# Edge groups visited in twos, windows stored as 24 rows, and the last chunk's node sums formed on chip, in a graph layer on one core

## The chip, the cores and the metric

The kernel runs on one core of one Trainium2 chip. The core has a matrix engine (TensorE, PE in the profile; its weight loads are PEld), a vector engine (VectorE, DVE), an activation engine (ScalarE, ACT), a general engine (GpSimd, POOL), a queue engine (SyncE, SP) and 16 DMA engines that all queues share. Each engine carries out its own instructions in the order in which they stand; between engines there are semaphores. DMAs are issued on the queues of SP, ACT and POOL. The metric is the device time of one execution in microseconds.

## The reference, cut to what matters

```python
xn = layernorm(x)                                   # 10000 nodes x 512, fp32
# graph part: 160000 edges, sorted by dst
h = xn @ W
agg = segment_sum(h[src] * edge_weight[:, None], dst, num_segments=10000)
gnn = relu(agg + bias)
# mixing part: linear attention, 8 heads of 64
q, k, v = split(xn @ w_qkv.T)
q = softmax(q over the head's 64) * 64 ** -0.5      # k: softmax over the nodes
mix = layernorm((q @ (k.T @ v) per head) @ w_out.T) * gamma
x1 = x + gnn + mix
# feed-forward: 6 experts, one set of expert weights for the whole graph
r = router(mean over nodes of layernorm(x1))        # top 2 of 11 partitions
out = x1 + sum_e r[e] * (gelu(layernorm(x1) @ W1[e] + b1[e]) @ W2[e] + b2[e])
```

`dst` is 10000 u^2 for uniform u, so low node numbers have many edges and high ones few. The sum over edges is formed before the product with W, on rows of xn: segment_sum(w * xn[src]) @ W.

## The kernel before

**Chunks.** The nodes are held in NCH = 20 chunks: 19 of 512 rows (128 partitions x SUB = 4 rows) and a last one of 272 (68 partitions x 4). KB = 4 blocks of 128 columns make up the 512.

**Start (0 to about 160 us).** SP loads the chunks of x (`normal_rows`, L416). DVE makes their statistics (L166, L167), POOL and ACT finish and apply them (L422), and ACT stores the rows to `xn_d` in DRAM (L424). After LISTS = 10 chunks the edge lists are loaded, and `place_edges` (a generator of DVE steps) works out which window and row every edge belongs to; two of its steps are taken after each further chunk. Meanwhile PE forms keys and queries of chunks 0 and 1 (L209), DVE their softmax (L192 to L194) and the sums G = xn.T ek (L912, L919). Rows of chunks from 2 on are reloaded from `xn_d` (`rows_of`, L835).

**Edges.** The 160000 edges are NET = 1250 tiles of 128. A window of up to 32 rows (WIN) takes the sums of one tile (of two for the first PAIRED = 384 windows), since tiles of edges sorted by dst touch few nodes. GROUP = 4 windows share one PSUM bank: a group's matmuls (L602) have 32 columns of weights each, side by side, and give `pm` of 128 rows. `edges_in` issues a group's gathers on POOL (L584, 128 rows of xn_d each) and makes its selection matrices on DVE (L590, L592). `edges_summed` does the matmuls, the copy out of PSUM on ACT (L605) and one store of 256 KB to `part_d` on ACT's queue (L606). There are 217 groups (NQ) and buffers for 24 tiles. Two windows that share nodes are joined by `carry` (L674, a DMA that adds in DRAM), chained over stretches whose ends are CARRIES.

**Order of the work.** The order on PE is written out by hand. Between blocks of other matmuls `work(us)` is told how long the block takes, and calls `edges_to` with the number of groups that a fixed rate (PACE, then ROW_PACE) allows by then. `edges_to` first issues gathers ahead (AHEAD, then LATE tiles) and then does the visits. The order on the other engines comes from a scheduler, with ties where the code says `behind(a, b)`.

**Stage 1 (to about 1092 us)** makes keys, queries and G for chunks 2 to 19, with seven products in place of eight (L243), edge groups between. A branch for unusual edge lists follows (`general_path`, not taken here), and the small product that mixes heads.

**Stage 2 (about 1115 to 1906 us).** For every chunk: `attention` (po = q times G, L209, kept as `ot`), then `gathered(c)`, which fetches the chunk's summed rows from part_d by the list `row_of` (L1018 on POOL; a node without edges takes a row of zeros), their transposes (L201, aT), and pg = aT times W (L209). DVE adds the bias, applies relu, adds to `ot` (L1090, L1091) and makes statistics for the feed-forward part; `ot` is stored to x1_d. Attention runs MIXED = 3 chunks ahead. `far_enough` has AT_HAND, which says how many windows must be done and carried before a chunk's rows may be fetched; the last two chunks wait for all edges. At chunk 17 `all_edges_in` does the rest of the edges and the last carry, and loads the experts' weights; DVE then forms w_sum (L226 to L229). After chunk 18 the first rows of the feed-forward part are loaded, normalised (L351 on ACT), transposed (L367 on DVE) and summed to xs (L233 to L236).

**Feed-forward (about 1906 us to the end)** is a long run of L243 products, with sums on DVE and gelu on ACT (L1277, L1290 to L1297).

Of the kernel before, what the change touches and what calls it, by code (L numbers as in the profile page):

```python
# [17 lines left out]
P = 128  # L18
SQ = 32
# [7 lines left out]
WIN = P // GROUP  # L27
FAR = 1.0e5
EARLY = 2
ROWS_IN = 1.6  # L30
LISTS = 10
# [5 lines left out]
LATE = 4  # L37
MIXED = 3

AT_HAND = [(5, 320), (7, 384), (8, 424), (9, 472), (10, 520), (11, 560), (12, 604), (13, 640), (14, 680), (15, 716), (16, 752),  # L40
           (17, 788), (18, 820)]
# [11 lines left out]
]  # L53


@with_exitstack
def gps_layer_kernel(
# [91 lines left out]
    ZERO_ROW = NQ * P  # L149
# [38 lines left out]
    def softmax_rows(q, r, s):  # L188
# [5 lines left out]
        nc.vector.tensor_tensor(q3, q3, qs[:r, :, None].to_broadcast([r, D // HEAD, HEAD]), ALU.mult)  # L194
# [29 lines left out]
    def sums_of(o, a11, a12, a21, a22):  # L224
# [4 lines left out]
        nc.vector.tensor_tensor(o[3], a12, o[1], ALU.subtract)  # L229
# [149 lines left out]
    def sums_of_weights():  # L379
        w1_sb, w1_sum = held_w["w1"], held_w["w1_sum"]  # L380
        p_half, q_half = slice(0, PAIRS * P), slice(PAIRS * P, 2 * PAIRS * P)
        sums_of([w1_sum[:, i] for i in range(4)], w1_sb[:, :KH, p_half], w1_sb[:, KH:, p_half],
# [5 lines left out]
    with ExitStack() as ph:  # L388
# [18 lines left out]
        normal = []  # L407
        placing = []
        last_stats = [None]

        def normal_rows(n):

            for c in range(len(normal), min(len(normal) + n, NCH)):
                r = chunks[c][1]
                xt = (xp if c < KEPT else a_io).tile([P, SUB, D], F32, name="xn")
                nc.sync.dma_start(xt[:r], tokens(x, c))  # L416
# [11 lines left out]
                for _ in range(2 if placing else 0):  # L428
                    next(placing[0], None)
# [10 lines left out]
        count = ep.tile([P, 3 + len(AT_HAND) + 2 * NCH], F32, name="count")  # L440
        small_norms = ep.tile([P, 2, KB], F32, name="small_norms")
        usable = ep.tile([P, 1], F32, name="usable")
        n_odd = ep.tile([1, 1], I32, name="n_odd")

# [9 lines left out]
        def place_edges(dst_sb, row_sb):  # L454


            nc.vector.tensor_scalar(row_sb, row_sb, 2, None, op0=ALU.arith_shift_right)
            yield
# [12 lines left out]
            def by_window_of(t, per_window, o, op):  # L471
# [27 lines left out]
            nc.vector.scalar_tensor_tensor(place, place, float(SUB), good, op0=ALU.add, op1=ALU.subtract)  # L499
            yield  # L500
            nc.vector.scalar_tensor_tensor(good, place, float(SUB), beyond, op0=ALU.is_lt, op1=ALU.is_equal)
            yield
            nc.vector.scalar_tensor_tensor(good, place, float(WIN), good, op0=ALU.is_lt, op1=ALU.mult,
                                           accum_out=count[:, 0:1])
# [3 lines left out]
            nc.vector.scalar_tensor_tensor(good[:, : NW - 1], gap[:, : NW - 1], float(WIN // SUB), good[:, : NW - 1],  # L508
                                           op0=ALU.is_lt, op1=ALU.mult, accum_out=count[:, 1:2])
# [14 lines left out]
        def window_at(node, more):  # L524
            tile_no = NET * (node / N) ** 0.5 + more
            return min(max(int(tile_no / 2 if tile_no < 2 * PAIRED else tile_no - PAIRED), 0), NW)

        def span(c):
            return window_at(chunks[c][0], -SPARE), window_at(chunks[c][0] + SUB * chunks[c][1], SPARE)
# [153 lines left out]

        done = [0, 0.0]
        pace = [PACE]
        ahead = [AHEAD]
        EARLY_TOTAL = PRODUCT * KB * ROWS_IN * 3 * KB

        def edges_to(stop):
# [784 lines left out]
```

## Time and profile before

| what | us |
|---|---|
| median of 3 runs | 3501.84 (3490.08 to 3503.91) |
| the profiled execution | 3295.9, of it the span 3294.2 |
| PE busy | 3187.5 (97%) |
| DVE busy | 1772.1 (54%) |
| POOL busy | 1317.8 (40%) |
| ACT busy | 834.1 (25%) |
| mean granted PE clock | 0.985 of full |

The span is from the first to the last instruction of the profiled execution. The profiled execution took 206 us less than the median of the runs. A busy PE counts from start to modelled end of its records, so 97% says that it rarely stood still, not that it did as much as it could. A record is one pass; a matmul in fp32 leaves two. In a list of waits, the idle time of an engine is put down to the instruction whose semaphore came last. A DMA-issuing line on POOL or ACT shows the time of issue, not that of the transfer.

### The profile page before, as it was taken

Reading aid. Unit: us, or ns where it says so; the run is one execution under the profiler, and the core shown is the slowest. Engines: PE = TensorE matmul, PEld = TensorE weight load, DVE = VectorE, ACT = ScalarE, POOL = GpSimd, SP = SyncE. Lnnn points to the kernel's source line nnn. Section 1 sums busy time; section 2 is a strip of 40 time slices with the busy share of each in tenths; the row PEclk is TensorE's granted clock in tenths of the full one; section 3 lists DMA queues with packets and bytes.
Section 4 is the critical chain, followed back from the end, with each engine's and each line's share of the span. In section 5 each row is a group of like instructions: output and inputs, shape, how many; then the busy total and the mean of one; then the engine's idle time right before and its main releaser. Section 6 shows DMA issues by size and latency. Waiting matters only on the chain. (4 is left out here: it accounts for less than half of the span.)

```text
span 3294.2 us, 35223 instructions
## 1 busy us (share of the span) xinstructions
PE 3187.5 (97%) x12819; PEld 1898.0 (58%) x12819; DVE 1772.1 (54%) x3902; ACT 834.1 (25%) x1674; POOL 1317.8 (40%) x1421
## 2 busy tenths in 40 slices
PE   5899999999999999999999979999999999999998
PEld 3344444444443333333333358888888888888886
DVE  6655555555555366666665665455544554445532
ACT  5422222222222122222222132222222222222211
POOL 3377777777776777777777200000000000000000
PEclk8899999999999999999999989999999999999999
DMA  9678889888888999999999822121212212121111
GB/s 391 245 238 282 265 274 311 265 281 255 283 267 240 344 353 355 337 350 351 354 338 313 230 67 62 52 90 52 64 52 76 66 52 64 52 90 51 54 38 41
DMA packets 216728, 654.33 MB, mean 199 GB/s; under 512 B 34425, under 2 KB 74361, under 8 KB 188831
## 3 DMA queue, kind: packets, MB, share of 16 engines
q0 software_dynamic: 104096, 354.29, 32.9%
q1 hardware_dynamic: 69992, 175.33, 16.2%
q10 hardware_dynamic: 42452, 122.31, 9.6%
q8 instruction: 105, 1.72, 0.2%
q14 instruction: 83, 0.68, 0.1%
HBM read 491.21 MB, written 166.63 MB: 200 GB/s over the span
## 5 line engine op out<-in xcount | busy, mean ns | idle before, releaser
L584 POOL DMA_INDIRECT msg<-xn_d,src_sb x1250 | 1237.6, 990 | 422.9 <-issue 318.4
L602 PE MATMUL pm<-msg,sel 128*32 128x512 f32 x2504 | 357.7, 604 | 15.4 <-DMA msg<-xn_d,src_sb 14.4
L209 PE MATMUL pg<-wq,aT 128*128 128x512 f32 (+1 forms) x640 | 292.2, 604 | 0.0
L209 PE MATMUL po<-G,qT 128*128 128x512 f32 (+1 forms) x640 | 290.3, 600 | 1.4 <-DMA qT<-qT_d 1.4
L912 PE MATMUL pc<-xn,ek 128*128 128x512 f32 (+1 forms) x640 | 285.5, 596 | 0.0
L605 ACT COPY part<-pm 128x512 f32<-128x512 f32 x217 | 127.0, 585 | 618.3 <-PE pm L602 577.4
L602 PEld LDWEIGHTS pm<-msg,sel 128*32 128x32 f32 x2504 | 67.0, 109 | 273.0 <-issue 190.5
L209 PEld LDWEIGHTS pg<-wq,aT 128*128 128x128 f32 (+1 forms) x640 | 115.5, 188 | 176.1 <-issue 161.2
L243 PE MATMUL px<-xnT,w_sb 128*128 128x256 f32 (+1 forms) x800 | 204.9, 379 | 7.0 <-DVE u L1291 6.6
L209 PEld LDWEIGHTS po<-G,qT 128*128 128x128 f32 (+1 forms) x640 | 114.8, 187 | 164.7 <-issue 157.8
L166 DVE BATCH_NORM_STATS2 st<-ot 128x6 f32<-128x512 f32 (+1 forms) x160 | 110.4, 690 | 180.1 <-ACT ot L1053 179.3
L243 PE MATMUL p<-kq_sum,xs_b 128*128 128x512 f32 (+1 forms) x432 | 200.7, 600 | 0.0
L912 PEld LDWEIGHTS pc<-xn,ek 128*128 128x128 f32 (+1 forms) x640 | 118.0, 191 | 139.3 <-issue 131.4
L243 PE MATMUL px<-w_sb,hh 128*128 128x256 f32 (+1 forms) x800 | 185.8, 379 | 0.0
L243 PE MATMUL py<-xs,w_sum 128*128 128x256 f32 (+1 forms) x800 | 185.7, 375 | 0.0
L243 PE MATMUL py<-w_sum,hh 128*128 128x256 f32 (+1 forms) x800 | 179.2, 379 | 0.0
L243 PEld LDWEIGHTS px<-xnT,w_sb 128*128 128x128 f32 x800 | 150.8, 192 | 30.1 <-DVE u L1291 10.2
L243 PEld LDWEIGHTS px<-w_sb,hh 128*128 128x128 f32 (+1 forms) x800 | 150.2, 188 | 22.8
L243 PEld LDWEIGHTS py<-w_sum,hh 128*128 128x128 f32 (+1 forms) x800 | 150.0, 188 | 22.7
L243 PEld LDWEIGHTS py<-xs,w_sum 128*128 128x128 f32 x800 | 150.2, 191 | 20.1
L243 PEld LDWEIGHTS p<-kq_sum,xs_b 128*128 128x128 f32 (+1 forms) x432 | 78.0, 187 | 116.1 <-issue 89.6
L351 ACT ACTIVATE xn<-xn,st_all 128x128 f32<-128x128 f32 x288 | 114.8, 481 | 97.3 <-DMA xn<-x_d 97.3
(298 smaller groups left out, 4566.8 us busy)
## 6 DMA issues: line engine op xcount, KB each, us to landing
part_d<-part ACTq DMA_DIRECT2D x217, 256.0 KB
msg<-xn_d,src_sb POOLq DMA_INDIRECT x1250
xn<-in_x SPq DMA_DIRECT2D x19, 1024.0 KB
xn_d<-xn ACTq DMA_DIRECT2D x19, 1024.0 KB
qT_d<-qT ACTq DMA_DIRECT2D x19, 1024.0 KB
qT<-qT_d SPq DMA_DIRECT2D x19, 1024.0 KB
xt<-in_x SPq DMA_DIRECT2D x19, 1024.0 KB
x_d<-ot SPq DMA_DIRECT2D x19, 1024.0 KB
```

The source lines that it names most:

```text
L166: nc.vector.bn_stats(st[:r, s, :], t[:r, s, :])
L209: nc.tensor.matmul(po[:r, :], t[:, kb, s * r : (s + 1) * r], w[:, kb, :], start=kb == 0, stop=kb == KB - 1)
L243: nc.tensor.matmul(o, lhs[j], rhs[j], start=start and j == 0, stop=stop and j == n - 1, skip_group_check=True)
L351: nc.scalar.activation(xn[:, s, b * P : (b + 1) * P], xn[:, s, b * P : (b + 1) * P], AF.Identity, bias=st[:, b, s, 0:1], scale=st[:, b, s, ...
L584: nc.gpsimd.indirect_dma_start(out=m[k], out_offset=None, in_=xn_d, in_offset=bass.IndirectOffsetOnAxis(ap=src_sb[:, t0 + k : t0 + k + 1], ...
L602: nc.tensor.matmul(pm[h * WIN : (h + 1) * WIN, :], sel[:, k, :], m[k] if k < len(m) else m[0], start=j == 0, stop=j == batch - 1, skip_gro ...
L605: nc.scalar.copy(part, pm)
L912: nc.tensor.matmul(pc, ek[:r, s, cb * P : (cb + 1) * P], xn[:r, s, :], start=s == 0, stop=s == SUB - 1)
```

## The change

Three constants change the edges' rhythm, and two others their limits.

- **Visits in twos.** In stage 2 `edges_to` is called for a multiple of VISIT = 2 groups, and gathers are issued LATE = 8 tiles ahead instead of 4. `limit` holds back the last groups until their place at chunk 17.
- **24 rows stored.** In stage 2 each window's first USED = 24 rows are stored, by four DMAs a group in place of one. `rest_cleared` fills rows 24 to 31 of those windows with zeros once, by 16 stores on ACT's queue early in stage 1. The check of the lists (`place_edges`) now asks for 24 rows in these windows.
- **The last chunk's sums on chip.** Groups from ON_CHIP = 211 on keep their sums in SBUF (`parts`). `last_sums` adds them up for the last chunk, already transposed: a matmul of the parts with 0/1 matrices `mine`, which say which of the last 272 nodes each row belongs to (`numbered`, from an iota on POOL and DVE comparisons with `node_of`, which `nodes_on_chip` makes). What windows before 211 x 4 hold of those nodes is fetched from part_d as before and added in by small matmuls. Only groups up to STORED = 214 are still stored. The last carry (to the last window) goes, and a carry at window 853 is added to AT_HAND for chunk 18.
- **Order at the end of stage 2.** The last chunk's attention comes in its turn. Chunk 17's pg, two visits, the first 16 of the matmuls of `last_sums`, and the last visit follow each other; the gathers of chunks 18 and 19 are tied behind the last gather of edges. Loads of the first feed-forward rows and of the experts' weights move to the end of chunk 17; `sums_of_weights` moves to the end of chunk 18, and the last chunk's additions are tied behind it.
- **Order at the start.** The edge lists are loaded after LISTS = 18 chunks asked for. The first step of `place_edges` is tied behind the last statistics, and the step that ends the places is tied behind the last softmax of chunk 1; the steps are no longer dealt out between chunks. The reload of chunk 2 is tied behind the last load of x.

In the built order, stage 2 has 63 visits (60 of 8 tiles, 2 of 16, 1 of 12) in place of 118 (111 of 4, 5 of 8, one of 16, one of 24). Stage 1's visits and the feed-forward products are the same.

```diff
+USED = 24
-LISTS = 10
+LISTS = 18
-LATE = 4
+LATE = 8
+VISIT = 2
+FIRST_SUMS = 4
-           (17, 788), (18, 820)]
+           (17, 788), (18, 820), (19, 853)]
...
+    ON_CHIP = window_at(N, NET, chunks[-1][0], -3) // GROUP
+    STORED = -(-CARRIES[-1] // GROUP)
...
-                for _ in range(2 if placing else 0):
-                    next(placing[0], None)
...
-            part = pools["w"].tile([P, D], F32, name="part")
+            if i < ON_CHIP:
+                part = pools["w"].tile([P, D], F32, name="part")
+            else:
+                if (i - ON_CHIP) % 3 == 0:
+                    parts.append(io.tile([P, 3, D], F32, name="parts", tag="qT"))
+                part = parts[-1][:, (i - ON_CHIP) % 3, :]
             nc.scalar.copy(part, pm)
-            nc.scalar.dma_start(part_d[i * P : (i + 1) * P, :], part)
+            if batch > 1:
+                nc.scalar.dma_start(part_d[i * P : (i + 1) * P, :], part)
+            elif i < STORED:
+                for h in range(GROUP):
+                    nc.scalar.dma_start(by_window[i * GROUP + h, :USED, :], part[h * WIN : h * WIN + USED, :])
...
+        def rest_cleared():
+            zero = pools["w"].tile([P, PER, D], F32, name="none", tag="on", bufs=1)
+            nc.gpsimd.memset(zero, 0.0)
+            for w in range(PAIRED, STORED * GROUP, P):
+                end = min(w + P, STORED * GROUP)
+                for q in range(USED, WIN, PER):
+                    nc.scalar.dma_start(by_window[w:end, q : q + PER, :], zero[: end - w])
...
-            edges_to(groups_of(int(done[1] / pace[0])))
+            stop = min(groups_of(int(done[1] / pace[0])), limit[0])
+            edges_to(done[0] + (stop - done[0]) // visit[0] * visit[0])
...
+            if c == KEPT:
+                behind(load, last_load[0])
...
-                for _ in placing[0]:
-                    pass
+                for step in placing[0]:
+                    if step:
+                        behind(step, last_softmax[0])
...
+                behind(next(placing[0]), last_stats[0])
...
         def all_edges_in():
             edges_to(NQ)
-            carry(CARRIES[-1], NW - 1)
+            ats.append(gathered(NCH - 2))
+            ats.append(gathered(NCH - 1))
...
+            rows_first = rows_in(0)
             experts_weights()
...
+        def numbered():
+            b, r = chunks[-1]
+            mine = io.tile([P, NQ - ON_CHIP + 1, SUB, r], F32, name="mine", tag="xt", bufs=1)
+            number = mine[:, NQ - ON_CHIP]
+            nc.gpsimd.iota(number, pattern=[[1, SUB], [SUB, r]], base=b, channel_multiplier=0,
+                           allow_small_or_imprecise_dtypes=True)
+            for g in range(NQ - ON_CHIP):
+                nc.vector.tensor_scalar(mine[:, g], number, node_of[:, g : g + 1], None, op0=ALU.is_equal)
+            return mine
+
+        def last_sums(o, mine, groups, at):
+            n = SUB * chunks[-1][1]
+            for kb in range(KB):
+                kbs = slice(kb * P, (kb + 1) * P)
+                pt = psum.tile([P, SUB * P], F32, name="pt", tag="ps")[:, :n]
+                for g in groups:
+                    nc.tensor.matmul(pt, parts[g // 3][:, g % 3, kbs], mine[:, g].rearrange("p s n -> p (s n)"),
+                                     start=g == groups[0], stop=at is None and g == groups[-1], skip_group_check=True)
+                if at is None:
+                    nc.scalar.copy(o[:, kb, :n], pt)
+                    continue
+                r = chunks[-1][1]
+                for s in range(SUB):
+                    nc.tensor.matmul(pt[:, s * r : (s + 1) * r], at[:r, s, kbs], ident[:r, :r],
+                                     start=False, stop=s == SUB - 1, skip_group_check=True)
+                nc.vector.tensor_tensor(o[:, kb, :n], o[:, kb, :n], pt, ALU.add)
...
+            behind(sums, held["asked"])
...
-            if c + MIXED < NCH - 1:
+            if c + MIXED < NCH:
                 mixed.append(attention(c + MIXED, nodes_rows))
-            elif c == NCH - 3:
-                mixed.append(attention(NCH - 1, nodes_rows))
+            elif c < NCH - 1:
+                nodes_rows()
             else:
-                nodes_rows()
+                last_sums(aT, mine, range(FIRST_SUMS, NQ - ON_CHIP), at)
...
+            if c == NCH - 3:
+                limit[0] = ON_CHIP + FIRST_SUMS
...
+                if c == NCH - 1:
+                    behind(added, weights_summed)
...
             if c == NCH - 3:
-                sums_of_weights()
+                mine = numbered()
+                aT_last = io.tile([P, KB, SUB * P], F32, name="aT_last", tag="ot", bufs=MIXED + 2)
+                edges_to(limit[0])
+                last_sums(aT_last, mine, range(FIRST_SUMS), None)
+                rows_first = all_edges_in()
             if c == NCH - 2:
...
-                turn = turned_in(0, rows_turned(0, xn))
+                turn = turned_in(0, rows_turned(0, rows_first))
+                weights_summed = sums_of_weights()
```

## The prediction

> **What bounds the kernel now.** I read the page's totals first, then the table of stretches, the groups, the timelines of PE and POOL where they stop, and the chain of waits.
>
> ```profile
> PE 3187.5 (97%) x12819; PEld 1898.0 (58%) x12819; DVE 1772.1 (54%) x3902; ACT 834.1 (25%) x1674; POOL 1317.8 (40%) x1421
> L584 POOL DMA_INDIRECT msg<-xn_d,src_sb x1250 | 1237.6, 990 | 422.9 <-issue 318.4
> L602 PE MATMUL pm<-msg,sel 128*32 128x512 f32 x2504 | 357.7, 604 | 15.4 <-DMA msg<-xn_d,src_sb 14.4
> ```
>
> Over the whole span PE is the bound. But 1250 gathers of 0.95 us, with 0.30 us of issue between, are 1563 us in one queue: from the first at 149.5 to the last at 1837.8 POOL does hardly anything else. In that stretch two resources are nearly balanced, and the stretches show where the second one wins (columns: us; busy time of PE, PEld, DVE, ACT, POOL; PE clock; DMA share; GB/s):
>
> ```profile
> 1115.00:1785.00 670.00, 666.69 (x2324) 252.16 (x2324) 411.63 (x1057) 151.68 (x289) 504.62 (x506) 1.00 0.96 347
> 1785.00:1846.00 61.00, 49.18 (x153) 14.66 (x152) 23.57 (x64) 9.39 (x18) 38.43 (x40) 0.89 0.87 286
> 1846.00:1906.00 60.00, 59.50 (x183) 25.97 (x181) 46.12 (x94) 8.38 (x20) 6.30 (x45) 1.00 0.71 183
> 1906.00:1927.00 21.00, 7.98 (x28) 6.75 (x29) 11.62 (x23) 8.57 (x20) 0.00 (x0) 0.67 0.71 175
> ```
>
> From 1785 PE runs dry; the last gather sets the end of stage 2. The timelines (start, length) show that end on POOL and PE:
>
> ```profile
> 1837.81 0.95 POOL L584 DMA_INDIRECT msg<-xn_d,src_sb  x1 [0.30 <-issue]
> 1852.12 0.96 POOL L674 DMA_DIRECT2D part_d<-part_d  x1 [13.36 <-DMA b_sb<-in_b_b]
> 1857.22 1.04 POOL L1018 DMA_INDIRECT at<-part_d,row_of  x1 [4.14 <-DMA part_d<-part_d]
> 1919.02 2.05 PE L243 MATMUL px<-xs,w_sum 128*128 128x256 f32 x4 [13.52 <-DVE xs L235]
> ```
>
> With P the end of the last gather (1838.8), stage 2 ended at 1905.5 = P + 66.7, all PE work, and then came a hole of 13.5 us. The waits of PE name the holes that the change touches:
>
> ```profile
> PE pm L602 <- DMA msg<-xn_d,src_sb: 14.4, 14, 2.6
> PE pt L201 <- DVE G L919: 13.6, 2, 13.2
> PE px L243 <- DVE xs L235: 13.5, 1, 13.5
> ```
>
> **What the Trainium skill says.** "TensorE: Matmul & The Clock Gate", section "Part 1: The HAM clock gate": after an idle window of about 3.4 us the PE clock halves until it has been busy again. The trace agrees: four px records took 2.05 us after the 13.5 us hole, 1.03 later. So a long stall costs about 2 us more. The same page, section "Architectural detail", calls the queues of ACT and DVE strict first in, first out; the trace agrees (L351 stood behind root L174 of the last chunk until 1908.3). "DMA: Bandwidth & Descriptors", section "Why a DMA increments its semaphore by 16 and not by 1", says that a DMA is spread over the largest number up to 16 that divides its slowest dimension: 68 rows use 4 engines. The trace agrees: loading the 68-partition chunk ran alone at 106 GB/s with 0.22 of the engines busy. So a 24-row store would use 12 engines, and four of them put 8 rows on each, as one 128-row store puts on sixteen. Those twelve are not relieved; no run here shows it.
>
> **The change, part by part.** Record times are from PE's timeline, start to start: a 512-column record 0.43 us (two per matmul, so 0.86), a transpose 0.11; a 272-column record by ratio 0.23. The order on each engine is that of the changed program as built.
>
> *Start.* In before, DVE's small place_edges operations stand among statistics, and G L919 came late: the 13.2 us hole at 87. Moved behind the last statistics, they let the softmax and G follow statistics of chunks 16 and 17, whose loads landed at 91 and 94. I get chunk 0 done 7.5 us earlier (4 to 11). The second half, about 7.5 us of DVE (1.44+1.46+1.5+0.6+1+0.5+0.9), now stands ahead of xs_b, which the first L243 needs: at 157.0 in before, needed at 159.6, so it is late by 3.5 to 5. Net -3.5 us (-8 to +3). The reload's tie costs nothing: it is ready 30 us before its transposes. Sixteen clearing stores (7.7 MB, at 370 GB/s 21 us of DMA, 16 issues of 0.33 to 0.5 us on ACT) fall into 131 to 165, where DMA is mostly idle; without that cover they would hold qT copies and PE by up to 6 us.
>
> *POOL.* It gains a memset and four early gathers, but the fifth waits for place_edges' last sums, about 156 to 159, beside 155.9 before. Before, it then filled its 24 buffers and waited 6.2 us for PE's first visits (185 to 220), which now come 3.5 us earlier. So P' = P - 3 (-8 to +6).
>
> *Pairs.* A visit of four tiles costs 1.19 us, one of eight 2.10, so each pair saves 0.29. Stage 2 goes from 118 visits to 63: -15.7 us of PE. *Last sums.* 24 matmuls x 0.456 + 16 x 0.224 - 16 small transposes = +13.4 us. Net -2.3 us of PE, and only where PE is the bound.
>
> *Stores.* 118 groups x 3 more ACT issues x 0.33 to 0.5 us is 117 to 177 us of ACT in 790; it was 23% busy there (151.7 of 670). Hidden by ACT's idle time, if the stores land soon enough (second rival).
>
> *End of stage 2.* `mine` begins with an iota on POOL, placed behind the last gather. DVE's first is_equal waits for it, and behind that on DVE stand the additions and ot of chunk 16's second and third quarters, whose PSUM buffers chunk 17's transposes and pg need. PE gets there after the visit of groups 211 and 212, while 14 gathers (14 x 1.255 = 17.6 us) still have to be issued: it arrives about 8 to 11 us too early. Call the iota's end I; the trace has none of this size, the nearest POOL work is 0.3 to 1.06 us, so I = P' + 1.2 (0.5 to 3). Then: DVE catches up 3.4; pg 6.9; visit 2.1; pg 6.9; 16 La1096 7.3; last visit 2.1: I + 28.7. Chunk 18's sums come last: their last needed store leaves at I + 12.7, lands 5.8 later (as before's last, 1846.3 to 1852.1), then carry 5.1, gather 1 + 4 to 8: I + 28.6 to 32.6, a wait of 0 to 4, I take 1.5. Then transposes 1.75, pg 13.7, pst 0.9, sums 7.2, pg 13.7 = 37.3. One slow-clock stretch adds 2. End = P' + 1.2 + 28.7 + 1.5 + 37.3 + 2 = P' + 70.7, against P + 66.7: +4 (-2 to +12). The work now after the last visit is 30 us shorter; the stall takes that.
>
> *FFN start.* From T, the end of chunk 18's pg: normalising on ACT ends T+7.7, DVE's transposes T+11.6, xs T+14.8, three of four w_sum (1.48 each) T+19.2. PE works until T+22.6, so the 13.5 us hole closes. But the last chunk's additions stand behind w_sum: 8 x 0.64, statistics 3 + 1.4, gate rows 1.9 after T+20.7 or PE's last pg; u is done at T+32.8, and px's third product needs it. So that product starts 10.2 us after the last pg, in before 20.8 (1905.5 to 1926.3), a slow clock and its growth included: -9.7 after 0.9 for the clock (-13 to -3).
>
> Sum: -3 + 4 - 9.7 = -8.7 on 3295.9 us (span 3294.2): 3287. The runs have a median of 3501.84, 206 us above the profiled execution. If that is fixed, the same -8.7 gives 3493. If it is a slower PE, POOL's stalls shrink, and -3.5 - 2.3 - 9.7 gives 3486. I take 3493.
>
> **Rivals.** *Faster: PE, not POOL, sets stage 2.* If gathers run 20 us earlier, the iota is early and pairs pay: before's 1115.2 to 1905.5 less 51.5 us that its visits took beyond 1.19 and 2.10 is 738.8 of PE work; 736.5 from 1111.7, with the 27 us of such waits that came before 1750 and 1.5 for the last sums, ends at 1876.7. With the FFN start that is -38: 3464. For it: in 1100 to 1840 POOL waited 19.6 us (43 times) for earlier gathers, at 0.96 DMA share, and stored bytes fall by a quarter. Against it: the 12 engines, and POOL's rate of 39 to 40 gathers in 50 us was the same at 0.83.
>
> *Slower: stores hold ACT.* Each store waits for the one eight before it, the same store of the previous pair, about 10.5 us back. Copies of pm, aT and po stand behind it on ACT; pm has two buffers. The decisive point is a landing beyond 10.5 us: alone it was 5.8, carries under load took 7 to 11. An excess of 0.8 us in 60 visits is 48, less about 17 of slack that PE has against POOL: +31 - 8.7, so 3524. For it: DMA's 0.96 and 12-engine stores; against: ACT's idle 77%.
>
> *No effect at all of the FFN part* (weights landing late, w1 being loaded behind the last visit): -8.7 + 9.7 gives 3503; it lies inside my range.
>
> **How the numbers follow.** No change can be told from one within about 0.5%, 17.5 us. Likeliest case 0.42 (with its late-weights form), own range 3481 to 3507: 0.05 of it faster. Faster rival 0.38, 3450 to 3484, of it 0.03 same. Slower rival 0.20, 3505 to 3545, of it 0.02 same. Faster 0.05 + 0.35 = 0.40; same 0.37 + 0.03 + 0.02 = 0.42; slower 0.18. The range, 3458 to 3522, leaves out a tenth of each end.
>
> **What would show it.** Right: PE idle 8 to 11 us on DVE ot before chunk 17's pg; the last gather near 1836; stage 2's end about 71 us after it; no hole ahead of the first px, one of about 5 us ahead of its third product; the hole at 87 near 6, and one of 4 at the first L243. Wrong: is_equal finding its iota done; the last gather before 1820 or after 1850; msg waits spread through stage 2; ACT's DMA issues waiting ahead of copies.

## The result, and the profile after

The changed kernel took 3526.2 us (median of 22 runs, 3493.1 to 3547.7); the kernel before, run beside it, 3489.9 (22 runs, 3457.2 to 3508.1). The ratio is 1.0084, 95% interval 1.0063 to 1.0105: slower by about 29 us. (The ratio is formed from fast runs alone, without the two longest executions of the changed kernel; the medians of all runs lie 36 us apart.) The forecast was 3493, range 3458 to 3522.

One thing must be known to read any number below: chips came in two kinds. In the later comparisons the kernel before took 3492 to 3495 us on three chips and 3298 on two, every one of its 20 to 59 runs on a chip within 1% of that chip's median. The profile that the prediction was read from (3295.9) looks like the quick kind, the timed runs beside it (3490 to 3504) like the slow kind. The comparison above is of the slow kind. Each of the five chips was measured at one time only, so the kind may also be a state in which the chip was then.

From the page of the changed kernel: engine totals, and two groups.

```profile
PE 3274.2 (93%) x12883; PEld 1942.7 (55%) x12883; DVE 1773.1 (50%) x3930; ACT 826.3 (23%) x1674; POOL 1314.0 (37%) x1423
...
L594 POOL DMA_INDIRECT msg<-xn_d,src_sb x1250 | 1236.1, 989 | 654.8 <-issue 333.4
L612 PE MATMUL pm<-msg,sel 128*32 128x512 f32 x2504 | 355.3, 612 | 39.4 <-issue 29.1
```

The span is 3527.1 us. The gathers take what they took before (0.99 us each). POOL was idle ahead of them for 655 us, where the profile behind the prediction has 423. But most of that comes with the kind of chip and not with the change, as the page of the kernel before on a chip of the slow kind shows (b_again, below):

```profile
L584 POOL DMA_INDIRECT msg<-xn_d,src_sb x1250 | 1232.4, 986 | 625.3 <-issue 339.6
```

On the slow kind POOL does not set the pace, with or without the change. The list of waits of the changed kernel says for whom it waited, and how PE stood still (total, times, longest):

```profile
PE pt L211 <- issue: 32.4, 36, 3.8
PE pm L612 <- issue: 29.1, 35, 1.5
PE po L219 <- issue: 20.5, 19, 5.4
PE pg L219 <- issue: 20.3, 12, 6.0
...
PE pt L211 <- DVE G L973: 8.6, 1, 8.6
...
POOL msg L594 <- PE pm L612: 145.0, 51, 12.0
```

POOL waited 145 us for PE to give buffers back (110 in b_again). In the trace that the prediction used, PE's waits in stage 2 were for gathers (14.4 us); here they are many waits with no releaser shown ("issue"), spread over transposes, visits and products. The four groups listed come to 102 us; the same four come to 67 in b_again. The hole for G has shrunk from 13.2 to 8.6, as the start of the change meant.

The end of stage 2, from the timelines of POOL and PE (start, length):

```profile
2071.49 0.95 POOL L594 DMA_INDIRECT msg<-xn_d,src_sb  x1 [0.30 <-issue]
2072.45 0.39 POOL L1084 IOTA mine<- 128x272 f32 x1
...
2073.89 0.81 PE L211 MATMUL pt<-ident,at 128*128 128x128 f32 x4 [3.17 <-issue]
2080.95 8.88 PE L219 MATMUL pg<-wq,aT 128*128 128x512 f32 x16 [6.25 <-ACT aT L213]
...
2156.98 2.07 PE L253 MATMUL px<-xnT,w_sb 128*128 128x256 f32 x4 [4.88 <-DVE u L1380]
```

The iota stands behind the last gather, and PE is held for 3.2 and 6.3 us ahead of chunk 17's pg. The last pg ended at 2146.9, and the third px product began 10.1 us later.

Against an execution of the kernel before on a chip of the same kind (span 3492.4), stage by stage from the PE timelines:

| stretch | before | after | difference |
|---|---|---|---|
| first L243 (L253 after) product starts at | 159.4 | 157.1 | -2.3 |
| stage 1, to the first po | 1116.4 | 1118.0 | +1.6 |
| stage 2, first po to the last pg's end | 829.5 | 871.8 | +42.3 |
| last pg to the third px product | 21.6 | 10.1 | -11.5 |
| from there to PE's end | 1354.1 | 1359.1 | +5.0 |

The start and the beginning of the feed-forward part moved about as forecast. The loss is in stage 2.

### The profile page after: what moved, and what is told of

Read it like the earlier page. It is cut to its first block, busy times and chain, and to the rows that moved or that the text cites. A ratio compares the mean times of both kernels' runs of the same rounds, so it can differ in the third digit from the quotient of the medians.

```text
span 3527.1 us, 35757 instructions
## 1 busy us (share of the span) xinstructions
PE 3274.2 (93%) x12883; PEld 1942.7 (55%) x12883; DVE 1773.1 (50%) x3930; ACT 826.3 (23%) x1674; POOL 1314.0 (37%) x1423
## 3 DMA queue, kind: packets, MB, share of 16 engines
q0 software_dynamic: 104096, 354.20, 32.3%
## 5 line engine op out<-in xcount | busy, mean ns | idle before, releaser
L966 PE MATMUL pc<-xn,ek 128*128 128x512 f32 (+1 forms) x640 | 308.1, 631 | 22.2 <-ACT ek L951 10.1
L219 PE MATMUL po<-G,qT 128*128 128x512 f32 (+1 forms) x640 | 301.6, 616 | 25.1 <-issue 20.5
L219 PE MATMUL pg<-wq,aT 128*128 128x512 f32 x608 | 285.3, 619 | 29.1 <-issue 20.3
L219 PEld LDWEIGHTS pg<-wq,aT 128*128 128x128 f32 x608 | 114.9, 195 | 197.0 <-issue 171.1
L253 PE MATMUL px<-xnT,w_sb 128*128 128x256 f32 (+1 forms) x800 | 206.1, 381 | 11.7 <-DVE u L1380 11.7
L253 PE MATMUL p<-kq_sum,xs_b 128*128 128x512 f32 (+1 forms) x432 | 203.8, 605 | 5.8 <-DVE xs_b L238 3.4
L253 PE MATMUL px<-w_sb,hh 128*128 128x256 f32 (+1 forms) x800 | 185.7, 379 | 0.0
L253 PE MATMUL py<-xs,w_sum 128*128 128x256 f32 (+1 forms) x800 | 185.4, 375 | 0.0
L253 PE MATMUL py<-w_sum,hh 128*128 128x256 f32 (+1 forms) x800 | 179.2, 379 | 0.0
L253 PEld LDWEIGHTS px<-xnT,w_sb 128*128 128x128 f32 x800 | 151.0, 193 | 35.7 <-DVE u L1380 16.1
L253 PEld LDWEIGHTS py<-w_sum,hh 128*128 128x128 f32 (+1 forms) x800 | 150.1, 188 | 22.6
L253 PEld LDWEIGHTS px<-w_sb,hh 128*128 128x128 f32 (+1 forms) x800 | 150.1, 188 | 22.6
L253 PE MATMUL p<-wk,xnT 128*128 128x512 f32 (+1 forms) x288 | 142.4, 618 | 20.8 <-issue 12.3
L253 PEld LDWEIGHTS py<-xs,w_sum 128*128 128x128 f32 x800 | 150.1, 191 | 19.9
L600 DVE TENSOR_TENSOR sel<-iota_w,place 128x128 f32<-128x128 f32 (+2 forms) x217 | 73.3, 340 | 161.4 <-remote 67.4
```

Source lines behind the costliest of these rows:

```text
L219: nc.tensor.matmul(po[:r, :], t[:, kb, s * r : (s + 1) * r], w[:, kb, :], start=kb == 0, stop=kb == KB - 1)
L253: nc.tensor.matmul(o, lhs[j], rhs[j], start=start and j == 0, stop=stop and j == n - 1, skip_group_check=True)
L600: nc.vector.tensor_tensor(sel[:, :n], iota_w[:, None, :].to_broadcast([P, n, WIN]), place[:, t0 : t0 + n, None].to_broadcast([P, n, WIN]), ...
L966: nc.tensor.matmul(pc, ek[:r, s, cb * P : (cb + 1) * P], xn[:r, s, :], start=s == 0, stop=s == SUB - 1)
```

## The experiments

**Parts undone, on a chip of the slow kind (before 3493.4).** First the kernel before once more, for its profile:

> The kernel before, unchanged, for a second profile beside the first, whose 3295.9 us lies below every timed run. If the pauses of PE without a named cause belong to most executions of both kernels, this one shows a span near 3490, about 100 to 130 us of such pauses and POOL waiting for PE's visits by more than 100 us; if they come with the change, its span is near 3295 and there are none.

Measured: 3494.2. No execution near 3295 came again on this chip; the earlier profile was not typical of the runs that it was set beside. Set against each other, the two profiles of the kernel before differ only in the stretches with gathers: stage 1 took 1116.4 us here and 955.6 there, stage 2 829.5 and 790.3, while the time to the first L243 product (159.4 and 159.6) and the feed-forward part from its third product on (1354.1 and 1356.3) are the same.

a_visit1, single visits:

```diff
-LATE = 8
-VISIT = 2
+LATE = 4
+VISIT = 1
```

> The changed kernel with visits of one group and the old lookahead of 4 tiles (VISIT 1, LATE 4), all else kept. If visits in twos do what they are for, 55 more visits at 0.29 us make it 12 to 16 us slower than the changed kernel: ratio to before 1.012. If visits in twos are the cause of the loss (buffers come free in bursts, ACT gets eight stores at once), it is 15 to 30 us faster than the changed kernel: 1.000 to 1.004.

Measured: 3497.6, ratio to before 1.0015 (0.9990 to 1.0040). Single visits remove nearly all of the loss.

a_store1, windows stored whole, in one store a group:

```diff
-USED = 24
+USED = 32
-            if batch > 1:
+            if i < STORED:
                 nc.scalar.dma_start(part_d[i * P : (i + 1) * P, :], part)
-            elif i < STORED:
-                for h in range(GROUP):
-                    nc.scalar.dma_start(by_window[i * GROUP + h, :USED, :], part[h * WIN : h * WIN + USED, :])
...
-                rest_cleared()
```

> The changed kernel with one store of all 128 rows a group again (USED 32) and no clearing stores, all else kept. If stores in fours hold ACT's copies and through them PE, it is 15 to 30 us faster than the changed kernel: ratio 1.000 to 1.004. If ACT's idle time hides them, it is within 5 us of the changed kernel: 1.007 to 1.010.

Measured: 3520.6, ratio 1.0069 (1.0035 to 1.0102). Not told from the changed kernel, although the waits of ACT's copies of `part` for landing stores fell from 80 us to 10 in the profiles.

a_iota takes these lines from the end of stage 2 into `nodes_on_chip`, early in stage 1:

```diff
-            number = mine[:, NQ - ON_CHIP]
-            nc.gpsimd.iota(number, pattern=[[1, SUB], [SUB, r]], base=b, channel_multiplier=0,
-                           allow_small_or_imprecise_dtypes=True)
```

> The changed kernel with the iota of the last chunk's numbers made once at the start, in a tile of its own, so that DVE's comparisons no longer wait behind the last gather. By the prediction's step the two holes of 3.2 and 6.3 us ahead of chunk 17's pg go: 8 to 10 us faster than the changed kernel, ratio 1.006. If another wait (a gather, the carry for chunk 18) takes their place, under 3 us: 1.008.

Measured: 3519.2, ratio 1.0074 (1.0050 to 1.0097). Not told from the changed kernel. The stall behind the iota was worth 9 us in the profile of the changed kernel, but in that of a_iota PE still stands for 8.2 us at the same place: ACT's copies of aT come late, behind a copy of sums that starts at 2071.6, 10 us after its visit's records. On this kind of chip another wait stands ready where the iota's was, so the run does not show what the iota costs.

**What of the pairs costs, on another chip of the slow kind (before 3492.1).**

b_pairs puts the pairs alone into the kernel before:

```diff
-LATE = 4
+LATE = 8
+VISIT = 2
...
-            edges_to(groups_of(int(done[1] / pace[0])))
+            stop = groups_of(int(done[1] / pace[0]))
+            edges_to(done[0] + (stop - done[0]) // visit[0] * visit[0])
```

> The kernel before with visits in twos and gathers issued 8 tiles ahead, nothing else changed (windows stored whole, in one store a group). If twos by themselves cost the time, it is 20 to 28 us slower than before: ratio 1.006 to 1.008, and its stage 2 some 25 us longer than that of before. If twos cost only together with the 24-row stores or the new end of stage 2, it is within 8 us of before, and if the pairs' saving of 0.29 us a pair comes through, 10 to 16 us faster (0.996). My bet is 1.006.

Measured: 3509.9, ratio 1.0053 (1.0034 to 1.0073). Pairs alone, without the 24-row stores and the new end, cost 18 us. Stage 2 took 870.2 us in its profile, 829.5 in that of before; the profiled execution was the longest of the 22, so these 41 us overstate it.

c_visit1_late8 makes single visits and leaves LATE at 8:

```diff
-VISIT = 2
+VISIT = 1
```

> The changed kernel with single visits but with the gathers still issued 8 tiles ahead: it parts the two constants that the run with single visits changed together. If the look-ahead is what costs (rows of a chunk and carries stand behind four more gathers on POOL), it stays near the changed kernel: 1.006 to 1.008 of before. If the pairing of visits on PE costs, it is like the run with single visits: 0.999 to 1.004. My bet is 1.002.

Measured: 3497.0, ratio 1.0008 (0.9984 to 1.0032). It is not the longer look-ahead by itself.

c_store1_parts4 is a_store1 with a fourth buffer:

```diff
-                part = pools["w"].tile([P, D], F32, name="part")
+                part = pools["w"].tile([P, D], F32, name="part", bufs=4)
```

> The changed kernel with one whole store a group (visits still in twos) and four SBUF buffers for the copied sums in place of three. With three, the second copy of a pair waits for the landing of the first store of the pair before, one period of about 10.5 us back; with four it waits for a store two periods back, and nothing else on ACT waits for a store. Theory 1 (ACT is held by landing stores, and PE waits for the copies behind): 15 to 25 us less than with one store and three buffers (3520.6), so about 1.001 of before, and ACT's waits for stores ahead of the copies of sums, 80 us in the changed kernel, gone. Theory 2 (twos cost on PE whatever the stores do): 1.006 to 1.008 again. My bet is theory 2, 1.006.

Measured: 3511.7, ratio 1.0059 (1.0034 to 1.0083). With the waits for landing stores loosened in both places the loss stays, so they are not its main cause. Up to about 9 us of the 29 may be theirs; the intervals overlap.

c_all puts a_visit1, a_store1 and a_iota together.

> The changed kernel with single visits 4 tiles ahead, one whole store a group, and the iota made once at the start: what is left of the change is the start, the last chunk's sums on chip and the order of the end of stage 2. Single visits gave 1.0015 of before. The early iota takes away holes of 3.2 and 6.2 us on PE, of which 0 to 9 us come through, the single stores give 0 to 5: so 0.998 to 1.001, 0.999 most likely, a few us below the kernel before. If the start and the end of stage 2 cost more than the 11 us that the feed-forward's start gains, it stays at 1.0015 or above.

Measured: 3489.1, ratio 0.9999 (0.9977 to 1.0021). Start, last sums on chip and feed-forward start together give nothing on this kind of chip.

**What the pairs wait for.** The trace of the pairs alone on the slow kind shows it. One place in stage 2, PE first, then ACT, then DVE (start, length):

```profile
1817.70 1.92 PE L603 MATMUL pm<-msg,sel 128*32 128x512 f32 x16
1819.56 1.97 PE L202 MATMUL pt<-ident,at 128*128 128x128 f32 x16
1821.36 3.60 PE L210 MATMUL po<-G,qT 128*128 128x512 f32 x8
1834.73 2.08 PE L210 MATMUL pg<-wq,aT 128*128 128x512 f32 x2 [9.77 <-issue]
...
1821.47 0.58 ACT L606 COPY part<-pm 128x512 f32<-128x512 f32 x1 [2.30 <-PE pt L202]
...
1827.79 0.58 ACT L606 COPY part<-pm 128x512 f32<-128x512 f32 x1 [5.74 <-remote]
1834.09 0.58 ACT L204 COPY aT<-pt 128x512 f32<-128x512 f32 x1 [5.71 <-issue]
...
1821.47 0.29 DVE L591 TENSOR_TENSOR sel<-iota_w,place 128x128 f32<-128x128 f32 x1 [1.57 <-PE pt L202]
...
1827.79 0.29 DVE L591 TENSOR_TENSOR sel<-iota_w,place 128x128 f32<-128x128 f32 x1 [5.04 <-remote]
```

The pair's records lie at 1817.7 to 1819.6. ACT copies the first group out at 1821.47 and the second at 1827.79, idle in between; DVE, which waits for the same two groups to give back their selection matrices, starts in the same hundredths. So in this place it is not ACT or a store that is late, but what both of them see of PE. The transposes behind, whose records end at 1821.5, reach ACT at 1834.09, and PE stands for 9.8 us ahead of the pg that needs the copy. The Trainium skill, "Perfetto Trace Analysis", section "Tensor Engine Instruction (MATMUL, LD_WEIGHTS)", says that the end of a PE record is computed and the release of its semaphore is not in the record. This trace is in line with it, and puts a size on what can be hidden there: 8.2 us after the second group, 12.6 after the transposes. "Late release" below is the name of this gap. Whether the product itself ended late or only the news of it came late, the records cannot tell.

The next table pairs each copy of pm and po with its group's last record, for copies before which ACT was idle. Lateness is counted from about 0.45 us after that record's start, its pitch:

| trace | copies over 1 us late | latest, us |
|---|---|---|
| before, as profiled for the prediction | 0 of 281 | 0.6 |
| before, slow kind | 134 of 229 | 14.7 |
| single visits, slow kind (a_visit1, c_visit1_late8, c_all) | 127 to 146 | 15.4 to 16.2 |
| visits in twos, slow kind (after, b_pairs, a_store1, a_iota, c_store1_parts4) | 127 to 148 | 18.7 to 21.9 |
| before with the new feed-forward start, and with pairs, quick kind (b_ffn, b_pairs_2) | 0 of 282, 0 of 283 | 0.7 |
| the changed kernel, quick kind (a_again) | 56 of 274 | 4.8 |

Not every late copy is a late release: 37 of the 56 in a_again are put down to a store that had not landed, and so are 32 of the 148 in the changed kernel on the slow kind, but only 4 of the 127 in b_pairs. In b_again the late ones lie between 197 and 2046 us; its gathers run from about 150 to 2036.7, and such copies from 187 to 2061. In the feed-forward part of the same trace, after the gathers, ACT follows PE's products within 0.04 us (121 instructions before which it was idle). So the next question was whether the gathers make the lateness.

**The feed-forward start alone, and the gathers taken away, on a chip of the quick kind (before 3297.9).** b_ffn puts one part into the kernel before: the first rows loaded and `squares` made at the end of chunk 17, the rest as here.

```diff
             if c == NCH - 3:
-                sums_of_weights()
...
             if c == NCH - 2:
...
                 turn = turned_in(0, rows_turned(0, xn))
+                weights_summed = sums_of_weights()
...
+                if c == NCH - 1:
+                    behind(added, weights_summed)
```

> The kernel before with one part of the change alone: the order at the start of the feed-forward part (first rows loaded at the end of chunk 17, the sums of weights formed after chunk 18, the last chunk's additions behind them). The changed kernel's third px product came 10.1 us after the last pg, in the kernel before 21.6. If this gain stands by itself: 9 to 12 us below the kernel before, ratio 0.9965 to 0.9975. If loads of weights or the late additions of the last chunk take it back: 0.999 to 1.001.

Measured: 3288.6, ratio 0.9971 (0.9962 to 0.9979), 9.3 us. PE's timeline of b_ffn:

```profile
1917.38 1.03 PE L243 MATMUL px<-xs,w_sum 128*128 128x256 f32 x4
...
1923.75 1.13 PE L243 MATMUL px<-xnT,w_sb 128*128 128x256 f32 x4 [1.03 <-DVE u L1293]
```

The hole of 13.5 us is gone; the third product comes 6.2 us after the last pg at 1917.5. Part of the gain is given back just before: PE now stands for 6.1 us ahead of the last chunk's pg (from 1895.9 to 1902.0; b_ffn_2 has the same 6.1), because on ACT the normalising of the first feed-forward rows (L351, 1895.3 to 1901.7) stands ahead of the copies of aT that this pg needs. No run has the other order.

d_none has one block of zeros for all gathered rows, so the sums over edges are left out:

```diff
-                four_of = pools["m"].tile([P, GROUP, D], F32, name="msg")
+                if "msg" not in held:
+                    held["msg"] = pools["m"].tile([P, GROUP, D], F32, name="msg")
+                    nc.gpsimd.memset(held["msg"], 0.0)
+                four_of = held["msg"]
...
-                        nc.gpsimd.indirect_dma_start(
-                            out=m[k], out_offset=None, in_=xn_d,
-                            in_offset=bass.IndirectOffsetOnAxis(ap=src_sb[:, t0 + k : t0 + k + 1], axis=0))
```

> The kernel before with the 1250 gathers of edge rows left out: every visit multiplies one block of zeros that lies in SBUF, so the sums over edges are not computed; selection matrices, matmuls, copies, stores and the chunks' fetches stay. In ordinary executions ACT and DVE are released by PE's products up to 15 us after the products' records, from the first gathers to the last, and in the one exceptional execution never later than 0.6 us. Theory 1 (the gathers cause that delay): it is gone here, below 1 us, and the time is 3230 to 3290 us, ratio 0.925 to 0.942. Theory 2 (the delay comes with the products themselves or with visits): it stays at up to 15 us, and the time is 3440 to 3490.

Measured: 3237.8. d_none_pairs is the same with the edit of b_pairs:

> The same without gathers, visits in twos. With gathers, twos cost 0.5% (18 us). If that loss comes out of the delayed releases or of the gathers' transfers, the saving of 0.29 us a pair must show here: 12 to 18 us less than single visits without gathers. If twos cost through what stands on PE, ACT and DVE alone, they are 10 to 20 us slower here too.

Measured: 3215.8, so 22.0 us less than single visits, a little more than expected. Without gathers pairs pay.

d_rows loads 128 consecutive rows in place of the indexed ones, so the sums are of other rows:

```diff
-                        nc.gpsimd.indirect_dma_start(
...
+                        at_row = (t0 + k) * 37 % (N // P) * P
+                        nc.gpsimd.dma_start(m[k], xn_d[at_row : at_row + P, :])
```

> The kernel before with each gather by indices replaced by a plain load of 128 consecutive rows of the same buffer, of the same size and on the same queue of POOL; the sums over edges are those of other rows. It parts the indices from the traffic. If the traffic or POOL's issuing of transfers delays the releases: 3470 to 3500 us and releases up to 15 us late. If it is the gathering by indices: 3280 to 3320 us and releases within 1 us. My bet is the traffic.

Measured: 3242.1, 4 us more than no gathers at all. On this chip releases are prompt with the indexed gathers too (b_ffn: never over 0.7 us), so the run can't part indices from traffic as a cause of lateness; that stays open. It does show that on the quick kind what the indexed gathers cost, some 55 us, is not the bytes: the queue moved the same 354.29 MB in the same 104096 packets as in b_ffn. The pace of issue is the likely reason. An indexed gather took 0.99 us and 0.30 until the next; a plain load took 0.56, and POOL then waited 707 us for PE.

**The change and the pairs on a second chip of the quick kind (before 3297.7).** a_again is the changed kernel as it is, the other three repeat edits.

> The changed kernel as it is, on another chip. On a chip where the kernel before takes about 3298 us and releases are prompt, the prediction's own sum stands to be tested (-8.7 us, 3287 against its profiled 3295.9): 3270 to 3295, ratio 0.992 to 0.999. On a chip where the kernel before takes 3490, 1.0084 again.

Measured: 3295.2, ratio 0.9991 (0.9984 to 0.9998).

> The kernel before with visits in twos alone. Where releases are prompt POOL's gathers set the end of stage 2, and the pairs' saving on PE is hidden: 0.998 to 1.002. If twos cost in themselves: 1.005 here too. On a chip with late releases 1.0053 again.

Measured: 3294.5, ratio 0.9987 (0.9979 to 0.9994). The same program that costs 0.53% on the slow kind gains 0.13% here. The same place as above (the 175th copy of a group), PE and ACT:

```profile
1608.77 4.17 PE L603 MATMUL pm<-msg,sel 128*32 128x512 f32 x16
1612.87 1.97 PE L202 MATMUL pt<-ident,at 128*128 128x128 f32 x16
...
1609.98 0.59 ACT L606 COPY part<-pm 128x512 f32<-128x512 f32 x1 [0.52 <-PE pm L603]
...
1612.97 0.59 ACT L606 COPY part<-pm 128x512 f32<-128x512 f32 x1 [2.41 <-PE pm L603]
1613.56 0.59 ACT L204 COPY aT<-pt 128x512 f32<-128x512 f32 x1
```

The copies follow the records within 0.6 us, and no copy in this trace is over 0.6 us late.

> Without gathers, single visits. On a quick chip 3238 us again. On a slow one: if gathers make the late releases, releases within 1 us in stage 2 and 3230 to 3290 us; if not, 3400 or more.

Measured: 3238.9.

> Without gathers, visits in twos. On a quick chip 3216 us again, 22 below single visits. On a slow one: the same 15 to 25 us below single visits if the gathers make the pairs' loss; above them if the chip itself does.

Measured: 3217.3; pairs save 21.6 us again.

**Without gathers on a third chip of the slow kind (before 3495.0).**

> Without gathers, single visits (the sums over edges are not computed). On a chip where the kernel before takes 3490 us: if the gathers make the late releases, releases within 1 us in stages 1 and 2 and 3230 to 3290 us, ratio 0.925 to 0.943; if the chip is late by itself, 3400 us or more. On a quick chip 3239 us, 0.982, again.

Measured: 3238.5, ratio 0.9261 (0.9230 to 0.9293): the same time as on the quick kind. From its page:

```profile
PE 3141.9 (97%) x12819; PEld 1890.1 (58%) x12819; DVE 1768.0 (55%) x3902; ACT 833.5 (26%) x1674; POOL 82.9 (3%) x172
...
L602 PE MATMUL pm<-msg,sel 128*32 128x512 f32 x2504 | 314.2, 604 | 3.7 <-ACT part L605 3.7
```

Four copies in 255 are over 1 us late, the latest by 4.5, as in d_none, where three of them wait for a store. Without gathers the lateness goes, and with it the whole difference between the kinds of chip: gathers cost 256 us here and 59 on the quick kind. The visits of this run also multiply zeros, and no run parts that from the missing gathers; but the products of stage 1 keep their data, and in b_again they were late too.

> The kernel before with the order at the start of the feed-forward part alone. On the quick chip it was 0.9971 of before, 9.3 us. That stretch has no gathers, so on a slow chip the same 8 to 12 us should come: 0.9965 to 0.998. If the late releases of the last chunks take it back: 0.999 to 1.002.

Measured: 3484.9, ratio 0.9969 (0.9954 to 0.9984). This one part gains 9 to 11 us on both kinds. It is the best version found: before with the new feed-forward start alone, 0.997 of before on either kind, against 1.0084 (slow kind) and 0.9991 (quick kind) for the whole change.

## Why the prediction was wrong

**The step that failed** is the last one of the sum: "If that is fixed, the same -8.7 gives 3493." The 206 us between the profiled execution and the runs were not a fixed amount laid over the same schedule. They came with late releases of PE's products, and under these the term "so each pair saves 0.29" turned round: the pairs cost 18 to 24 us. The stretches of the two profiles of the changed kernel, slow kind and then quick kind, hold nearly the same work (PE records in brackets first):

```profile
1280.00:2030.00 750.00, 677.94 (x2336) 267.32 (x2335) 409.91 (x1054) 146.35 (x289) 504.18 (x505) 0.95 0.88 297
```

```profile
1120.00:1790.00 670.00, 656.47 (x2330) 263.38 (x2328) 415.56 (x1065) 149.73 (x289) 506.45 (x508) 1.00 0.95 337
```

The same 2330 records took 80 us more, with a lower DMA share: neither POOL nor the DMA engines were the limit. Of the 80, 59 are idle time of PE and 21 longer busy time, at a mean granted clock of 0.95 in place of 1.00. In stage 1 of the kernel before the same shows: 1012 us busy in place of 948, at 0.95 in place of 1.00. Whether the lower clock only follows from PE's pauses was not tested; without gathers it is 1.00 on the slow kind as well (d_none_3, both stages). The other branch that the text weighed, a slower PE under which POOL's stalls shrink (3486), was nearer in that POOL does stop being the bound, but it priced pairs as a gain.

**What the chip of the slow kind did, term by term**, against 3490 us: pairs +24 (after less a_visit1; +18 when put into before), the feed-forward start -11 (b_ffn_2), start and last sums together about +10 (c_all less b_ffn_2), stores and iota together about +6 (a_visit1 less c_all, within its uncertainty). The sum is +29, but it has to be: each term is the difference of two neighbouring versions, so the sum proves nothing, and their uncertainties are 5 to 12 us. The +10 fits the prediction's own +13.4 for the last sums, unhidden where POOL is not the bound, less 2.3 for the start; no run had the last sums alone.

**Why late releases cost more in twos** is shown only so far: pairs lose on the slow kind, gain on the quick kind, and gain 22 us without gathers (on the quick kind; there is no such pair of runs on the slow kind). The latest release is later in all five traces with twos than in the five with single visits. PE's stalls over 1 us in stage 2 came to 54 to 83 us in the five with twos and to 27 to 51 in the five with single visits (b_again, a_visit1, c_visit1_late8, c_all, b_ffn_2). That two groups and the transposes behind them hang on late releases one after the other is how I read the example; no run took that apart.

**On the quick kind the same steps can be checked one by one.** Timelines of the changed kernel there, POOL and PE:

```profile
1835.02 0.94 POOL L594 DMA_INDIRECT msg<-xn_d,src_sb  x1 [0.30 <-issue]
1835.97 0.41 POOL L1084 IOTA mine<- 128x272 f32 x1
...
1837.43 0.66 PE L211 MATMUL pt<-ident,at 128*128 128x128 f32 x4 [4.46 <-DVE ot L1183]
1844.49 9.06 PE L219 MATMUL pg<-wq,aT 128*128 128x512 f32 x16 [6.40 <-ACT aT L213]
...
1875.17 3.15 PE L211 MATMUL pt<-ident,at 128*128 128x128 f32 x16 [3.52 <-DMA at<-part_d,row_of]
...
1924.40 2.07 PE L253 MATMUL px<-xnT,w_sb 128*128 128x256 f32 x4 [4.88 <-DVE u L1380]
```

- *Start:* the hole for G is 8.7 (forecast near 6), the one at the first L253 product 3.4 (forecast 4), the gain 2.9 us (forecast 3.5). Right in the main.
- *POOL:* the last gather ends at 1836.0, 2.8 us earlier (forecast 3). In agreement, but so close by luck: in b_ffn, whose gathers are those of before, the last one ended at 1844.5. The pairs' saving is largely hidden behind the gathers (b_pairs_2 gained 3 us).
- *End of stage 2:* the stall ahead of chunk 17's pg is 4.5 + 6.4 = 10.9 us (forecast 8 to 11, on DVE behind the iota). Right. But stage 2 ends at 1914.3, 78.3 us after the last gather, where 70.7 was forecast. DVE's catching up takes 8.1 us from the iota's end to the first pg in place of 3.4 (+4.7); the wait for at is 3.5 in place of 1.5 (+2.0); from there to the end 39.1 in place of 37.3 (+1.8); the iota 0.4 in place of 1.2 (-0.8). The blocks between the first pg and the wait for at took 27.2, which is the forecast 25.3 and the 2 of a slow clock.
- *Feed-forward start:* 10.1 us, forecast 10.2. Right. 3.4 us of it are lost again further on in this execution (1359.7 against 1356.3).
- *Sum:* -8.7 was forecast; -2.5 in the medians, and the span is 3295.0 against 3294.2. The mis-sized term is the end of stage 2.
- *A reading:* the DMA share during the load of the 68-partition chunk is 0.25 (124 to 129 us), not 0.22. That is four engines of sixteen, as the prediction wanted it.

**The rivals.** "Slower: stores hold ACT" gave 3524, near the measured 3526, by luck: most of the loss is there without its stores (b_pairs, a_store1). The waits of the changed kernel on the quick kind:

```profile
PE pm L612 <- DMA msg<-xn_d,src_sb: 14.4, 14, 2.6
...
PE pm L612 <- ACT part L620: 0.7, 1, 0.7
...
ACT part L620 <- DMA part_d<-part: 112.5, 40, 10.8
...
POOL msg L594 <- PE pm L612: 9.2, 20, 3.4
```

Stores do hold ACT, 40 times and 112 us, but PE waits 0.7 us for it: hidden by ACT's idle time, as the prediction said. "Faster: PE, not POOL, sets stage 2" was half true on the slow kind: PE did set it, but not at the pitch of its records. "No effect at all of the FFN part" fell: it is worth 9 to 11 us on both kinds.

## What to carry to other kernels

Where a profiled execution and the timed runs differ by several per cent, find out what the difference is made of before adding a change to either; a second profile of the unchanged kernel would have shown here that POOL waits for PE in stage 2. Measure how long after a product's last record its consumer starts, since a wait on a late release is listed as "issue" or "remote" and a group's busy time does not show it. Batching that saves on the pitch of records can lose when releases are late, as the pairs did; the edit whose gain lies outside the stretch with gathers held on both chips where it was tried.

## What the runs showed of the hardware

- On chips of the slow kind ACT and DVE saw PE's products up to 14.7 us late in the kernel before while gathers of edge rows ran, and up to 21.9 in versions with pairs; on the quick kind never more than 0.7 us (b_ffn, b_pairs_2). The kernel before takes 3492 to 3495 us on the one kind and 3298 on the other; without gathers it takes 3238 on both. What makes the chips differ was not found, nor whether it is the indices or the traffic.
- PE's granted clock went with it: in stage 1 of the kernel before it was 0.95 on the slow kind and 1.00 on the quick kind, and 1.00 on the slow kind without gathers.
- 1250 loads of 128 consecutive rows on POOL's queue cost 4 us over no loads at all on the quick kind; as many loads of the same size by index cost 60.
